# Inverses on distinct values by small DRAM transfers, two additions by accumulating transfers, output weights in one load

## Chip, cores and metric

One NeuronCore of a Trainium2 chip runs the whole kernel. The metric is the device time of one launch in microseconds, as the median over runs. Everything is computed in float32 (apart from a few bfloat16 helpers that carry a shift exactly).

## What is computed

One transformer block with conditioned RMS norms, and its input added once more at the end. x is 4 x 1024 x 512 (4 batches, 4096 tokens), cond is 4 x 128; 16 heads of 32.

```python
def norm(x, t, gw, gb, bw, bb):          # g and b come from the condition
    g = (t @ gw.T + gb)[:, None, :]
    b = (t @ bw.T + bb)[:, None, :]
    return g * x * rsqrt(mean(x * x, -1) + 1e-6) + b

a = norm(x, cond, g1w, g1b, b1w, b1b)
q, k, v = a @ Wq.T, a @ Wk.T, a @ Wv.T   # 16 heads of 32
p = softmax(q @ k.T / sqrt(32))
x2 = x + (p @ v) @ Wo.T
f = norm(x2, cond, g2w, g2b, b2w, b2b)
h = x2 + (silu(f @ gate_w.T) * (f @ hid_w.T)) @ out_w.T
out = x + h
```

## The kernel before, in words

**Layout.** Features lie on the 128 partitions (C = 4 chunks of 128), tokens along the free axis. The 4096 tokens are 8 blocks of 512; a batch is two blocks. A group hg of four heads fills 128 partitions.

**Rounds and units.** The main loop (`while g < NR + 10 ...`) runs rounds g. 256 of them begin a piece of attention: a *unit* j is 256 queries of one head group, and takes UN = 4 rounds, in each of which the scores of 256 keys are made. A block has 8 units, so 32 rounds. `kind` is g % 4. The pieces of one unit follow each other through later rounds: in round r `scores` writes PSUM (one buffer of four banks) and `keep` copies it to SBUF on ACT (tile raw, 9 buffers); `running_max` on DVE; after the fourth, `max_T` (PE, same PSUM buffer as scores), `parts`, `parts_T`, the copy mT on ACT and `spread` turn the maximum over keys into a tile `shift`. Five rounds after r, `shifted` (DVE) and `exponential` (ACT) make the weights; six rounds after, `weighted` multiplies them with v on PE into one PSUM tile av, and `accumulate` adds raw to the unit's first raw by a DMA issued on POOL (three per unit, 1 MB each). So for the last piece of a unit exponential is in kind 0 and accumulate in kind 1. `take_av` copies av to SBUF on ACT in kind 1; the next unit's `weighted` in kind 2 needs that PSUM tile again. In kind 3 `fold_sum` (DVE, L326) adds the two halves of the accumulated tile and `sums` adds over partitions on PE with a matrix of ones, which leaves each of the four heads' sums repeated on 32 partitions. One round later, in kind 0, `inverse` (DVE reciprocal, L341, 128x256) and `normalize` (L351) make oT.

**Chains.** All projections are cut into *chains*: four chunks accumulated in one PSUM tile of a pool of three, followed by an evict on ACT or DVE. There are 512: keys, queries and values of the next batches, the output projection (`project_out`), and per block 32 hidden chains and 16 contract chains of the feed-forward part. `first` holds the output projections with the round in which they are due, `queue` all others with the earliest round. A credit grows each round by 2.0 up to round BS + 16 and by PACE = 1.6 afterwards; a round takes a chain after `accumulate` and a second one (evicted in the next round) near its end, each where the credit is at least 1, something is due, or kind is 0. So a round has none, one or two chains; what is left when the rounds are over runs at the end without attention beside it.

**Order.** The program order of PE, DVE, ACT and POOL is the order of the calls in the loop. In a round it is: scores, the moved additions, the evict left from the round before, what is pinned to the round, spread, keep, exponential, weighted, accumulate, take_av, first chain, sums, running_max, evict, what is set `between`, max_T and parts in kind 0, second chain, parts_T, what is set `after`. All DMAs but the accumulates are issued on SP.

**Norms.** For a block of activations four squares (ACT), three additions (DVE), a matmul with ones/512 that leaves the mean square repeated on all 128 partitions, a square root (ACT, L124), a reciprocal of 128x512 on DVE (`norm_inverse`, L128), a multiplication per chunk (`norm_scale`, DVE) and the modulation (`norm_mod`, ACT). For batches after the first these are set a few rounds ahead of the round s in which the block's chains begin; for the feed-forward part at g0 + 9 to g0 + 16, where g0 is the first round after the block.

**Output projection.** `project_out` (L357) loads the output weights for two chunks at a time (twice per block, in the tag fw that the feed-forward weights use). Its evict adds the residual (L369, x2) and adds x2 to res (L370), into which the contract chains then add.

Of the kernel before, what the change touches and what calls it, by code (L numbers as in the profile page):

```python
# [10 lines left out]
F32 = mybir.dt.float32  # L11
BF16 = mybir.dt.bfloat16
AF = mybir.ActivationFunctionType
ALU = mybir.AluOpType
# [3 lines left out]
P = 128  # L18
NB = 512
# [5 lines left out]
def tile_cond_transformer_block(  # L25
# [12 lines left out]
    nc = tc.nc  # L38
    NBLK, _, C, _ = x.shape
    B = cond_t.shape[1]  # L40
    D = C * P
# [9 lines left out]
    UN = KT // 2  # L51
    RAW = 9
    PACE = 1.6
    SCALE = 1.0 / math.sqrt(DH)

    const = ctx.enter_context(tc.tile_pool(name="const", bufs=1))
# [34 lines left out]

    kq_s = {(b, hg): tc.dram_tile([P, 2, L], F32, name=f"kqs{b}_{hg}") for b in range(B) for hg in range(C)}
    v_s = [tc.dram_tile([P, C, KT, P], F32, name=f"vs{b}") for b in range(B)]


    columns = [P]

    def mm(dst, w, moving, start: bool, stop: bool):
        n = columns[0]
        for k in range(0, P, n):  # L100
            nc.tensor.matmul(dst[k : k + n, :], w[:, k : k + n], moving, start=start, stop=stop)  # L101
# [6 lines left out]
    def norm_squares(dst, tag: str, k: int):  # L108

        sq = [sb.tile([P, NB], F32, tag="t", name=f"sq{tag}_{2 * k + i}", bufs=3) for i in range(2)]  # L110
        for i in range(2):
            nc.scalar.activation(sq[i], dst[:, 2 * k + i, :], AF.Square)
        if k == 0:
            state[tag] = sb.tile([P, NB], F32, tag="tot", name=f"tot{tag}", bufs=1)
            nc.vector.tensor_tensor(state[tag], sq[0], sq[1], ALU.add)
        else:
            for t in sq:
                nc.vector.tensor_tensor(state[tag], state[tag], t, ALU.add)
# [5 lines left out]
        nc.scalar.activation(inv, pm, AF.Sqrt, bias=eps)  # L124
        state[tag] = inv

    def norm_inverse(tag: str):
        nc.vector.reciprocal(state[tag], state[tag])  # L128

    def norm_scale(dst, tag: str, c: int):  # L130
        nc.vector.tensor_tensor(dst[:, c, :], dst[:, c, :], state[tag], ALU.mult)
# [191 lines left out]

    def fold_sum(j: int):
        t = acc[j]
        nc.vector.tensor_tensor(t[:, :, 0, :], t[:, :, 0, :], t[:, :, 1, :], ALU.add)  # L326

    def take_av(j: int):
        avs[j] = sb.tile([P, HQ], F32, tag="avs", name=f"avs{j}", bufs=2)
# [2 lines left out]
    def sums(j: int):  # L332
        total = ps.tile([P, HQ], F32, tag="w", name=f"sum{j}")
        a = acc.pop(j)
        for i in range(HG):
            nc.tensor.matmul(total[i * DH : (i + 1) * DH, :], ones_sum, a[:, i, 0, :], start=True, stop=True)  # L336
        state["sum", j] = total

    def inverse(j: int):
        rec = sb.tile([P, HQ], F32, tag="rec", name=f"rec{j}", bufs=2)  # L340
# [12 lines left out]
    def load_res(n: int):  # L353
        res[n] = sb.tile([P, C, NB], F32, tag="b", name=f"res{n}", bufs=2)
        nc.sync.dma_start(out=res[n], in_=x[n])

    def project_out(n: int, d: int):  # L357

        if d == 0:
            x2[n] = sb.tile([P, C, NB], F32, tag="a", name=f"x2_{n}", bufs=3)  # L360
        if d % 2 == 0:
            wo[0] = sb.tile([P, C, 2 * P], F32, tag="fw", name=f"wo{n}_{d}", bufs=3)
            nc.sync.dma_start(out=wo[0], in_=vo_w[1][:, :, d * P : (d + 2) * P])
        pp = ps.tile([P, NB], F32, tag="w", name=f"po{n}_{d}")
        for c in range(C):
            mm(pp, wo[0][:, c, d % 2 * P : (d % 2 + 1) * P], oT[n, c], c == 0, c == C - 1)

        def evict():
            nc.vector.tensor_tensor(x2[n][:, d, :], pp, res[n][:, d, :], ALU.add)  # L369
            nc.vector.tensor_tensor(res[n][:, d, :], res[n][:, d, :], x2[n][:, d, :], ALU.add)  # L370

        return evict

    def load_f(n: int, f: int):
        t = sb.tile([P, 2, C, P], F32, tag="fw", name=f"fw{n}_{f}", bufs=3)
# [48 lines left out]
    def pin(g, fn, *a):  # L424
        pinned.setdefault(g, []).append((fn, a))

    def between(g, fn, *a):
        halfway.setdefault(g, []).append((fn, a))

    def after(g, fn, *a):  # L430
        ended.setdefault(g, []).append((fn, a))
# [20 lines left out]
        enqueue(0, (load_wkq, (hg,)), project_kq, (0, hg, 1, 1))  # L452
    for b in range(1, B):
        for half in range(QB):
            s = (len(queue) + 1) // 2
            if s > BS + 8:
                s += 2
            tag = f"a{b}_{half}"
            pin(max(s - 10, 0), load_y, b, half)
            for k in range(2):  # L460
                after(s - 8 + k, lambda b=b, half=half, tag=tag, k=k: norm_squares(y[b, half], tag, k))
            between(s - 6, norm_root, tag)
            after(s - 5, norm_inverse, tag)
            for c in range(C):
                between(s - 4, lambda b=b, half=half, tag=tag, c=c: norm_scale(y[b, half], tag, c))
                after(s - 4 + c // 2, lambda b=b, half=half, c=c: norm_mod(0, b, y[b, half], c))
            for load, fn, a in chains_of(b, half):
                enqueue(s, load, fn, a)
    for n in range(NBLK):
        g0 = (n + 1) * BS  # L470
        pin(g0 - 2, load_res, n)
        for d in range(C):
            first.append((g0 + 8, None, project_out, (n, d)))
        if n < NBLK - 1:
            tag = f"f{n}"
            for k in range(2):
                after(g0 + 9 + k, lambda n=n, tag=tag, k=k: norm_squares(x2[n], tag, k))
            between(g0 + 11, norm_root, tag)
            after(g0 + 13, norm_inverse, tag)
            for c in range(C):  # L480
                after(g0 + 14 + c // 2, lambda n=n, tag=tag, c=c: norm_scale(x2[n], tag, c))
            for c in range(C):
                after(g0 + 15 + c // 2, lambda n=n, c=c: norm_mod(1, n // QB, x2[n], c))
            g1 = g0 + 17
        else:
            g1 = 1 << 20
        for g in range(NF // FG):
            for k in range(FG):
                for a in range(2):
                    load = None if a else (load_f, (n, g * FG + k))  # L490
                    enqueue(g1, load, hidden, (n, g * FG + k, a))
            for d in range(C):
                enqueue(g1, None, contract, (n, g, d))
# [23 lines left out]
    with tc.manual_schedule(  # L517
# [32 lines left out]
                modulation(1)  # L550
        project_kq(0, 0, 0, 1)()

        late = None
        credit = 0.0
        g = 0
        while g < NR + 10 or pinned or ended:
            kind = g % UN
            r_x, r_v = g - UN - 1, g - UN - 2
            x_on, v_on = 0 <= r_x < NR, 0 <= r_v < NR
            j_m = g // UN - 1  # L560
            m_on = 0 <= j_m < NR // UN
            j_s = g // UN - 2
            s_on = 0 <= j_s < NR // UN
            j_n = g // UN - 3
            n_on = 0 <= j_n < NR // UN
            columns[0] = DH

            if g < NR:
                scores(g)
            if kind == 3 and s_on:  # L570
                fold_sum(j_s)
            if x_on and kind in (2, 3):
                shifted(r_x)
            if late is not None:
                late()
                late = None
            if kind == 0:
                if n_on:
                    inverse(j_n)
                if x_on:  # L580
                    shifted(r_x)
                if n_on:
                    normalize(j_n)
            for fn, a in pinned.pop(g, []):
                fn(*a)
            if kind == 1 and m_on:
                spread(j_m)
            if g < NR:
                keep(g)
            if kind == 1 and x_on:  # L590
                shifted(r_x)
            if x_on:
                exponential(r_x)
            if v_on:
                weighted(r_v)
                accumulate(r_v)
            if kind == 1 and s_on:
                take_av(j_s)
            credit = min(credit + (2.0 if g < BS + 17 else PACE), 2.9)
            due = bool(first) and first[0][0] <= g  # L600
            evict = None
            if credit >= 1 or due or kind == 0:
                evict = chain(g)
                credit -= evict is not None
            if kind == 3 and s_on:
                sums(j_s)
            if g < NR:
                running_max(g)
            if evict is not None:
                evict()  # L610
            if kind == 3 and g < NR:
                fold_max(g // UN)
            for fn, a in halfway.pop(g, []):
                fn(*a)
            if kind == 0 and m_on:
                columns[0] = P
                max_T(j_m)
                parts(j_m)
            if credit >= 1 or due or kind == 0:
                late = chain(g)  # L620
                credit -= late is not None
            if kind == 0 and m_on:
                parts_T(j_m)
            columns[0] = DH
            for fn, a in ended.pop(g, []):
                fn(*a)
            g += 1
# [63 lines left out]
```

## Time and profile before

| | us |
|---|---|
| median of 3 runs | 2547.93 (2547.44 to 2548.41) |
| the profiled execution: its own time | 2551.1 |
| its span, first to last instruction | 2549.3 |
| rounds begin, about | 48 |
| last scores begin | 2244 |

| groups on DVE that the change touches | count | mean ns |
|---|---|---|
| L341 reciprocal 128x256 | 64 | 1749 |
| L128 reciprocal 128x512 | 7 + 6 | 3345 |
| L326 fold of sums | 64 | 1214 |
| L370 res + x2 | 32 | 692 |

| transfers | count | KB | us from issue to landing, median |
|---|---|---|---|
| accumulate, issued on POOL | 192 | 1024 | 8.4 |
| fw, on SP | 128 | 512 | 4.2 |
| wo, on SP | 16 | 512 | 5.2 |
| out, on SP | 32 | 256 | 3.3 |
| condT, on ACT, at the start | 1 | 2 | 3.8 |

PE works in every slice of the span; the other engines' busy times are shares beside it. Shares are averages over a start (about 50 us), a stage in which the projections of later batches fill the rounds (to round 46), the blocks after it, and an end of about 240 us with the chains that are left. PE's gaps (the time between the end of all its matmuls so far and the next) and the stretches of half clock are read from single records; the waits say what ended them.

### The profile page before, as it was taken

The page shows a single profiled execution, that of the slowest core. Times are in us where ns is not written, and L with a number is a line of the kernel's source. Part 1 is how long each engine was busy: PE and PEld are TensorE (multiplying, and loading weights), DVE is VectorE, ACT ScalarE, POOL GpSimd, SP SyncE. Part 2 cuts the span into 40 slices and gives each one's busy share as a digit, 9 for nine tenths or more (in the row PEclk, how much of TensorE's full clock was granted, in tenths as well). Part 3 has the DMA queues.
Part 4 walks back from the last instruction along what each step waited for, and adds up shares of the span by engine and source line. Part 5 has one row for each costly group of instructions (what it writes and reads, how often), then busy time and mean ns, then how long its engine had stood idle before and what let it go on. Part 6 is the DMA issues. An engine that isn't in the chain of part 4 may idle for free. (4 is left out here: it accounts for less than half of the span.)

```text
span 2549.3 us, 51152 instructions
## 1 busy us (share of the span) xinstructions
PE 2473.6 (97%) x22976; PEld 1003.2 (39%) x22976; DVE 1803.1 (71%) x1600; ACT 1311.6 (51%) x1165; POOL 166.4 (7%) x200
## 2 busy tenths in 40 slices
PE   8999999999999998999999999999999999999999
PEld 3334344334433443344434433344334433433444
DVE  2566766777878787888887888788887878763211
ACT  3566775655555554655565555555555555541000
POOL 0000000000000000000000000000000000000000
PEclk9999999999999999999999999999999999999999
DMA  5678778767767775877677766877677766772221
GB/s 193 181 195 218 211 194 207 182 143 165 174 163 203 164 168 137 203 174 175 164 176 186 177 155 168 197 170 166 152 197 167 174 160 171 165 164 78 90 80 49
DMA packets 125931, 424.08 MB, mean 166 GB/s; under 512 B 12176, under 2 KB 36752, under 8 KB 99216
## 3 DMA queue, kind: packets, MB, share of 16 engines
q0 software_dynamic: 27648, 201.34, 41.0%
q1 hardware_dynamic: 97776, 219.45, 25.7%
q8 instruction: 181, 2.97, 0.5%
q14 instruction: 38, 0.31, 0.0%
q10 hardware_dynamic: 288, 0.01, 0.0%
HBM read 185.87 MB, written 33.55 MB: 86 GB/s over the span
## 5 line engine op out<-in xcount | busy, mean ns | idle before, releaser
L101 PE MATMUL ph<-x,fw 128*32 128x512 f32 (+1 forms) x6488 | 918.5, 595 | 6.7 <-DVE h L393 2.9
L289 DVE TENSOR_TENSOR raw<-raw,shift 128x2048 f32<-128x2048 f32 x256 | 581.3, 2271 | 108.8 <-ACT shift L285 108.8
L237 ACT COPY raw<-sc 128x2048 f32<-128x2048 f32 x256 | 479.4, 1873 | 320.8 <-PE sc L230 184.1
L294 ACT ACTIVATE raw<-raw 128x2048 f32<-128x2048 f32 x256 | 490.0, 1914 | 259.5 <-DVE raw L289 259.3
L101 PEld LDWEIGHTS ph<-x,fw 128*32 128x32 f32 (+1 forms) x6488 | 298.4, 118 | 511.6 <-issue 474.6
L101 PE MATMUL pc<-h,ow 128*32 128x512 f32 (+1 forms) x3184 | 460.6, 595 | 7.8 <-DVE h L395 5.4
L247 DVE TENSOR_TENSOR rmax<-rmax,raw 128x2048 f32<-128x2048 f32 x128 | 292.9, 2288 | 89.7 <-ACT raw L237 88.8
L318 POOL DMA_DIRECT2D raw<-raw x192 | 165.3, 861 | 2124.6 <-ACT raw L294 1303.3
L230 PE MATMUL sc<-kq 32*128 32x256 f32 x4096 | 295.3, 402 | 2.6 <-ACT raw L237 2.6
L304 PE MATMUL av<-raw,v 128*32 128x256 f32 x4096 | 277.8, 389 | 9.3 <-ACT raw L294 6.9
L101 PEld LDWEIGHTS pc<-h,ow 128*32 128x32 f32 (+1 forms) x3184 | 149.9, 118 | 259.8 <-issue 231.9
L230 PEld LDWEIGHTS sc<-kq 32*128 32x128 f32 x4096 | 185.9, 185 | 168.1 <-issue 132.7
L101 PE MATMUL pkq<-y,wkq 128*32 128x512 f32 (+1 forms) x1808 | 233.6, 600 | 9.6 <-DMA wkq<-in_kq_w 5.5
L393 DVE SCALAR_TENSOR_TENSOR h<-t,ph 128x512 f32<-128x512 f32 x128 | 88.0, 687 | 190.6 <-ACT t L391 190.6
L391 ACT ACTIVATE t<-ph 128x512 f32<-128x512 f32 x128 | 75.4, 589 | 219.9 <-PE ph L101 219.9
L407 DVE SCALAR_TENSOR_TENSOR res<-pc,res 128x512 f32<-128x512 f32 x128 | 88.0, 688 | 107.0 <-PE pc L101 106.9
L245 DVE TENSOR_TENSOR rmax<-raw,raw 128x2048 f32<-128x2048 f32 x64 | 146.2, 2285 | 24.4 <-ACT raw L237 24.4
L304 PEld LDWEIGHTS av<-raw,v 128*32 128x32 f32 x4096 | 108.2, 110 | 135.3 <-issue 48.7
L395 DVE TENSOR_TENSOR h<-ph,h 128x512 f32<-128x512 f32 x128 | 88.0, 688 | 68.8 <-PE ph L101 68.5
L101 PEld LDWEIGHTS pkq<-y,wkq 128*32 128x32 f32 (+1 forms) x1808 | 71.5, 115 | 143.2 <-issue 123.9
L101 PE MATMUL po<-oT,wo 128*32 128x512 f32 (+1 forms) x856 | 117.5, 605 | 10.2 <-DMA wo<-in_vo_w 6.0
L275 ACT COPY mT<-pt 12x256 bf16<-12x256 bf16 x64 | 23.1, 361 | 196.7 <-PE pt L273 196.7
(78 smaller groups left out, 1369.1 us busy)
## 6 DMA issues: line engine op xcount, KB each, us to landing
raw<-raw POOLq DMA_DIRECT2D x192, 1024.0 KB, 8.4
fw<-in_gh_w SPq DMA_DIRECT2D x128, 512.0 KB, 4.2
ow<-in_out_w SPq DMA_DIRECT2D x128, 256.0 KB, 4.8
wkq<-in_kq_w SPq DMA_DIRECT2D x32, 512.0 KB, 7.0
v<-vs SPq DMA_DIRECT2D x32, 512.0 KB, 5.8
kq<-kqs SPq DMA_DIRECT2D x31, 512.0 KB, 7.8
kqs<-st SPq DMA_DIRECT2D x61, 256.0 KB, 6.1
res<-in_x SPq DMA_DIRECT2D x8, 1024.0 KB, 6.5
```

Of the source, the lines that this page charges most:

```text
L101: nc.tensor.matmul(dst[k : k + n, :], w[:, k : k + n], moving, start=start, stop=stop)
L230: nc.tensor.matmul(sc[:, i, k, :], t[rows, kt * P : (kt + 1) * P], t[rows, q0 : q0 + HQ], start=True, stop=True)
L237: nc.scalar.copy(raw[r], state.pop(("sc", r)))
L245: nc.vector.tensor_tensor(rmax[j], raw[r - 1], raw[r], ALU.max)
L247: nc.vector.tensor_tensor(rmax[j], rmax[j], raw[r], ALU.max)
L289: nc.vector.tensor_tensor(t, t, shift[r // UN].unsqueeze(2).to_broadcast([P, HG, 2, HQ]), ALU.add)
L294: nc.scalar.activation(raw[r], raw[r], AF.Exp)
L304: nc.tensor.matmul(av[j][i * DH : (i + 1) * DH, :], v[m][:, kt, i * DH : (i + 1) * DH], raw[r][:, i, k, :], start=(kt == 0), stop=(kt == K ...
L318: nc.gpsimd.dma_start(out=acc[j].rearrange("p h k q -> p (h k q)"), in_=raw[r].rearrange("p h k q -> p (h k q)"), accum_op=ALU.add,)
L393: nc.vector.scalar_tensor_tensor(h[n, f], t, 1.0, pp, ALU.add, ALU.mult)
L395: nc.vector.tensor_tensor(h[n, f], pp, h[n, f], ALU.mult)
L407: nc.vector.scalar_tensor_tensor(r, pp, 0.5, r, ALU.mult, ALU.add)
```

## The change

The reciprocals are no longer taken on tiles in which each value is repeated on 32 or 128 partitions. Instead `compact` writes one row per head (or one row in all) to DRAM, `take` reads these values back spread over 128 partitions (8 or 4 per partition), `invert` takes their reciprocal on DVE, `put` writes them to DRAM, and `spread_inverse` reads them back repeated (four transfers for a unit, one for a norm). All of these are issued on ACT. For a unit, the sums are first copied from PSUM by ACT (kind 3), taken in kind 0 before keep, inverted and put at the end of kind 0, spread in kind 1 ahead of take_av, and `normalize` moves from kind 0 to kind 2. The last unit keeps the direct reciprocal, as do the first two norms and the last one.

`fold_sum` becomes an accumulating transfer on POOL in kind 2, behind `accumulate`. The addition of x2 to res becomes one accumulating transfer per block on POOL (`add_res`), but for the last block. The output weights of blocks 1 to 7 are loaded whole, seven rounds ahead, into tag a (three buffers, shared with y and x2). The credit grows by FIRST = 1.75 instead of 2.0, up to three rounds longer; output projections are due two rounds later, norms begin earlier ahead of s or later after g0, and feed-forward chains are let in at g0 + 20 instead of g0 + 17.

```diff
...
     PACE = 1.6
+    FIRST = 1.75
     SCALE = 1.0 / math.sqrt(DH)
...
     v_s = [tc.dram_tile([P, C, KT, P], F32, name=f"vs{b}") for b in range(B)]
+    inv_s = {}
...
-    def norm_inverse(tag: str):
-        nc.vector.reciprocal(state[tag], state[tag])
+    def compact(tag: str, t, rows: int, n: int):
+        inv_s[tag] = tc.dram_tile([P // rows, n], F32, name=f"sums{tag}")
+        nc.scalar.dma_start(out=inv_s[tag], in_=t[0:P:rows, :])
+    def take(tag: str):
+        src = inv_s.pop(tag)
+        few = sb.tile([P, src.shape[0] * src.shape[1] // P], F32, tag="few", name=f"few{tag}", bufs=2)
+        nc.scalar.dma_start(out=few, in_=src.rearrange("h (p c) -> (h p) c", c=few.shape[1]))
+        state["few", tag] = few
+    def invert(tag: str):
+        few = state["few", tag]
+        nc.vector.reciprocal(few, few)
+    def put(tag: str):
+        few = state.pop(("few", tag))
+        inv_s[tag] = tc.dram_tile(list(few.shape), F32, name=f"invs{tag}")
+        nc.scalar.dma_start(out=inv_s[tag], in_=few)
+    def spread_inverse(tag: str, t, rows: int, n: int):
+        src = inv_s.pop(tag).rearrange("(h p) c -> h (p c)", p=rows)
+        for h in range(P // rows):
+            nc.scalar.dma_start(
+                out=t[h * rows : (h + 1) * rows, :], in_=src[h : h + 1, :].to_broadcast([rows, n])
+            )
+    def norm_compact(tag: str):
+        compact(tag, state[tag], P, NB)
+    def norm_spread(tag: str):
+        spread_inverse(tag, state[tag], P, NB)
...
         t = acc[j]
-        nc.vector.tensor_tensor(t[:, :, 0, :], t[:, :, 0, :], t[:, :, 1, :], ALU.add)
+        nc.gpsimd.dma_start(out=t[:, :, 0, :], in_=t[:, :, 1, :], accum_op=ALU.add)
...
+    def sums_out(j: int):
+        t = sb.tile([P, HQ], F32, tag="rec", name=f"total{j}", bufs=2)
+        nc.scalar.copy(t, state.pop(("sum", j)))
+        compact(f"s{j}", t, DH, HQ)
+    def sums_in(j: int):
+        t = sb.tile([P, HQ], F32, tag="rec", name=f"rec{j}", bufs=2)
+        spread_inverse(f"s{j}", t, DH, HQ)
+        state["rec", j] = t
     def inverse(j: int):
...
+    def load_wo(n: int):
+        t = sb.tile([P, C, D], F32, tag="a", name=f"wo{n}", bufs=3)
+        nc.sync.dma_start(out=t, in_=vo_w[1])
+        for d in range(C):
+            wo[d] = t[:, :, d * P : (d + 1) * P]
     def project_out(n: int, d: int):
...
             x2[n] = sb.tile([P, C, NB], F32, tag="a", name=f"x2_{n}", bufs=3)
-        if d % 2 == 0:
-            wo[0] = sb.tile([P, C, 2 * P], F32, tag="fw", name=f"wo{n}_{d}", bufs=3)
-            nc.sync.dma_start(out=wo[0], in_=vo_w[1][:, :, d * P : (d + 2) * P])
+        if n == 0 and d % 2 == 0:
+            t = sb.tile([P, C, 2 * P], F32, tag="fw", name=f"wo{n}_{d}", bufs=3)
+            nc.sync.dma_start(out=t, in_=vo_w[1][:, :, d * P : (d + 2) * P])
+            for i in range(2):
+                wo[d + i] = t[:, :, i * P : (i + 1) * P]
         pp = ps.tile([P, NB], F32, tag="w", name=f"po{n}_{d}")
         for c in range(C):
-            mm(pp, wo[0][:, c, d % 2 * P : (d % 2 + 1) * P], oT[n, c], c == 0, c == C - 1)
+            mm(pp, wo[d][:, c, :], oT[n, c], c == 0, c == C - 1)
...
             nc.vector.tensor_tensor(x2[n][:, d, :], pp, res[n][:, d, :], ALU.add)
-            nc.vector.tensor_tensor(res[n][:, d, :], res[n][:, d, :], x2[n][:, d, :], ALU.add)
+            if n == NBLK - 1:
+                nc.vector.tensor_tensor(res[n][:, d, :], res[n][:, d, :], x2[n][:, d, :], ALU.add)
         return evict
+    def add_res(n: int):
+        nc.gpsimd.dma_start(
+            out=res[n].rearrange("p c q -> p (c q)"),
+            in_=x2[n].rearrange("p c q -> p (c q)"),
+            accum_op=ALU.add,
+        )
...
         for half in range(QB):
-            s = (len(queue) + 1) // 2
-            if s > BS + 8:
+            s = math.ceil((len(queue) + 1) / FIRST)
+            if s > BS + 11:
                 s += 2
             tag = f"a{b}_{half}"
-            pin(max(s - 10, 0), load_y, b, half)
+            pin(max(s - 11, 0), load_y, b, half)
             for k in range(2):
-                after(s - 8 + k, lambda b=b, half=half, tag=tag, k=k: norm_squares(y[b, half], tag, k))
-            between(s - 6, norm_root, tag)
-            after(s - 5, norm_inverse, tag)
+                after(s - 9 + k, lambda b=b, half=half, tag=tag, k=k: norm_squares(y[b, half], tag, k))
+            between(s - 7, norm_root, tag)
+            between(s - 7, norm_compact, tag)
+            after(s - 7, take, tag)
+            between(s - 6, invert, tag)
+            after(s - 6, put, tag)
+            between(s - 5, norm_spread, tag)
             for c in range(C):
...
         pin(g0 - 2, load_res, n)
+        if n:
+            pin(g0 + 3, load_wo, n)
         for d in range(C):
-            first.append((g0 + 8, None, project_out, (n, d)))
+            first.append((g0 + (10 if n < NBLK - 1 else 8), None, project_out, (n, d)))
         if n < NBLK - 1:
             tag = f"f{n}"
+            after(g0 + 12, add_res, n)
             for k in range(2):
-                after(g0 + 9 + k, lambda n=n, tag=tag, k=k: norm_squares(x2[n], tag, k))
-            between(g0 + 11, norm_root, tag)
-            after(g0 + 13, norm_inverse, tag)
+                after(g0 + 12 + k, lambda n=n, tag=tag, k=k: norm_squares(x2[n], tag, k))
+            between(g0 + 14, norm_root, tag)
+            between(g0 + 14, norm_compact, tag)
+            after(g0 + 14, take, tag)
+            between(g0 + 15, invert, tag)
+            after(g0 + 15, put, tag)
+            between(g0 + 16, norm_spread, tag)
             for c in range(C):
-                after(g0 + 14 + c // 2, lambda n=n, tag=tag, c=c: norm_scale(x2[n], tag, c))
+                after(g0 + 17 + c // 2, lambda n=n, tag=tag, c=c: norm_scale(x2[n], tag, c))
             for c in range(C):
-                after(g0 + 15 + c // 2, lambda n=n, c=c: norm_mod(1, n // QB, x2[n], c))
-            g1 = g0 + 17
+                after(g0 + 18 + c // 2, lambda n=n, c=c: norm_mod(1, n // QB, x2[n], c))
+            g1 = g0 + 20
         else:
...
+        direct = NR // UN - 1
         late = None
...
                 scores(g)
-            if kind == 3 and s_on:
-                fold_sum(j_s)
             if x_on and kind in (2, 3):
...
             if kind == 0:
-                if n_on:
+                if n_on and j_n >= direct:
                     inverse(j_n)
...
                 if n_on:
-                    normalize(j_n)
+                    if j_n >= direct:
+                        normalize(j_n)
+            if kind == 2 and n_on and j_n < direct:
+                normalize(j_n)
+            if kind == 0 and n_on and j_n < direct:
+                take(f"s{j_n}")
             for fn, a in pinned.pop(g, []):
...
                 accumulate(r_v)
+            if kind == 2 and s_on:
+                fold_sum(j_s)
+            if kind == 1 and n_on and j_n < direct:
+                sums_in(j_n)
             if kind == 1 and s_on:
                 take_av(j_s)
-            credit = min(credit + (2.0 if g < BS + 17 else PACE), 2.9)
+            credit = min(credit + (FIRST if g < BS + 20 else PACE), 2.9)
             due = bool(first) and first[0][0] <= g
...
                 sums(j_s)
+                if j_s < direct:
+                    sums_out(j_s)
             if g < NR:
...
                 parts_T(j_m)
+            if kind == 0 and n_on and j_n < direct:
+                invert(f"s{j_n}")
+                put(f"s{j_n}")
             columns[0] = DH
```

## Prediction

> **What bounds the kernel now.** I read the page first: which engine is full, and when.
>
> ```profile
> PE 2473.6 (97%) x22976; PEld 1003.2 (39%) x22976; DVE 1803.1 (71%) x1600; ACT 1311.6 (51%) x1165; POOL 166.4 (7%) x200
> ...
> PE   8999999999999998999999999999999999999999
> ...
> PEclk9999999999999999999999999999999999999999
> DMA  5678778767767775877677766877677766772221
> ```
>
> PE is busy 97% of the span of 2549.3 us and the change takes no matmul away, so only PE's empty time (71 us, its gaps added up) and clock lost after gaps (27 us, from the granted clock) can be won: 98 us. Next the windows, to see where these lie.
>
> ```profile
> 448.00:512.00 64.00, 58.58 (x610) 23.57 (x598) 49.64 (x39) 40.42 (x39) 4.30 (x5) 0.96 0.73 184
> ...
> 960.00:1024.00 64.00, 57.06 (x570) 22.72 (x567) 47.07 (x44) 33.53 (x27) 4.31 (x5) 0.95 0.58 130
> 1088.00:1152.00 64.00, 64.00 (x660) 26.33 (x656) 50.06 (x46) 35.80 (x29) 5.16 (x6) 1.00 0.76 176
> ```
>
> Columns: window, length, busy PE, PEld, DVE, ACT, POOL, clock, DMA share, GB/s. An ordinary stretch (the third) has no PE gap at all, though DVE is at 78%: there a faster DVE wins nothing. Gaps sit in the first 140 us, around round 48 (first line) and at block starts. The waits of PE and PEld name what ends them:
>
> ```profile
> PE pt L273 <- DVE split L268: 13.7, 9, 4.0
> PE po L101 <- DMA wo<-in_vo_w: 6.0, 1, 6.0
> ...
> PEld av L304 <- ACT avs L330: 16.7, 37, 2.0
> ```
>
> The last one is short each time but comes in 37 of 64 units: ACT's copy of avs is already just in time. The timelines of ACT, PE and POOL around one such round (kind 1, one chain) show it:
>
> ```profile
> 1194.63 1.92 ACT L294 ACTIVATE raw<-raw 128x2048 f32<-128x2048 f32 x1 [0.58 <-DVE raw L289]
> 1196.45 0.35 ACT L330 COPY avs<-av 128x256 f32<-128x256 f32 x1
> ...
> 1196.85 1.07 PE L304 MATMUL av<-raw,v 128*32 128x256 f32 x16
> ...
> 1170.91 0.86 POOL L318 DMA_DIRECT2D raw<-raw  x1 [13.74 <-ACT raw L294]
> 1179.23 0.86 POOL L318 DMA_DIRECT2D raw<-raw  x1 [7.46 <-ACT raw L294]
> 1188.46 0.86 POOL L318 DMA_DIRECT2D raw<-raw  x1 [8.37 <-DMA raw<-raw]
> ```
>
> The av starts 0.05 us after the copy ends, and POOL issues three accumulates per unit, each 8.4 us to landing. Last the packets: an accumulate's first packet runs 1.43 us after issue and its packets fill the engines 5.2 us when alone, 6.2 in the median. Of 199 SP transfers with nothing of SP's in front of them, 89 would have begun inside such a run; every one landed after the run's end. The other 110 took 3.5 us in the median, the smallest stores 2.3 (0.82 to the first packet, 0.66 after the last). **An accumulate shuts other transfers out**, and three fill some 60% of a unit.
>
> **The change, part by part** (us of PE time; gains negative).
>
> *Reciprocals, fold, residual off DVE.* 63 x 1.749 + 13 x 3.345 + 64 x 1.214 + 28 x 0.692 = 251 us, less 76 tiny reciprocals at 0.17 (the 128x8 rows): 238 of 1803. It counts where PE's gaps end on DVE: outside the items below, 20 us of gaps at block starts name DVE (split, h, res) and two dips in the clock (3.4 us at half) add 3.4: **-23**. Bounds 0 and -35 (all gaps there).
>
> *FIRST and the later due rounds.* Counting the credit rule through: before, rounds 47 and 48 find the queue empty (7.3 us of gaps and 13.65 us at half clock, 6.8): **-14**, bounds 0 and -14. Rounds without a chain are 74 and 234 before (kind 2, 3.4 each: 1.03 + 0.66 + half of 3.4); after, they are 10 (kind 2) and 109, 141, 173, which are kind 1, where avs has no slack: a missing chain of 3.6 uncovers some 3.3 and a dip adds 1.7. 3.4 + 3 x 5 - 6.8 = **+12**, bounds 5 and 25. 73 chains instead of 63 are left for the end, where one takes 3.43 instead of 3.62: **-2**.
>
> *Output weights whole*, seven rounds ahead: the one wait of 6.0 and its dip of 3.4 go, **-9** (bounds 0, -9).
>
> *take at kind 0.* ACT waits for compact's landing; behind it stand keep, exp and later mT. From the end of sums: copy and handover 0.6, first packet 0.82, landing 0.95, take's issue 0.5 (ACT's two transfers at the start held it 0.41 and 0.47): keep can start at 2.9, or 1.5 after the end of an accumulate that is running. Now it starts 1.2 after sums when kind 3 has one chain, 4.6 when it has two, and max_T comes 2.4 after keep's end; so 3.6 or 7.0 is free. Laid on the recorded accumulates, 16 of 61 units overrun, the longest by 5.5, together **+35**. Bounds 0 (accumulates do not block ACT's row) and 70 (take's read blocked as well).
>
> *put and four spread transfers before avs.* put goes out behind mT, usually into the third accumulate, and lands up to 4 us after kind 1's exp has begun. Four issues of 0.4 then stand in front of take_av; exp hides 1.8 of them. 36 of 62 units have no slack. Laid on the records: 26 units, together **+35**; bounds 0 and 70. At SP's shortest issue, 0.33, it is 6 less.
>
> *Dips.* Of these 42 waits 12 are over 2.2 us, and in the trace most gaps from 2.2 us on are followed by 3.4 us or more at half clock: **+20**, bounds 0 and 40.
>
> *fold_sum and add_res on POOL.* The third accumulate lands 4.3 to 22.4 us ahead of sums, 12 in the median. fold needs 1.43 to its first packet, half the bytes of an accumulate in pieces of 1 KB, some 3, and 0.7: 5.5 to 7.5, which overruns 2 or 3 units by 1.4 to 5.5 in all; if issuing grows fourfold with its 512 pieces, 10 us and some 20. The next accumulate stands behind it on POOL, with 14 us between them. add_res goes ahead of a third accumulate seven times (5.2 us, still inside 12). **+8**, bounds 1 and 30.
>
> *Norms' small transfers*: keep is held up to 6 us after the square root, but the next scores leave it 5.0 to 7.0. **0**; with that cover gone, 13 x 3. The copy out of sums holds the evict behind it on ACT by some 0.6 us and frees a PSUM buffer a round sooner: 0, covered by the three buffers. normalize waits on DVE for the spreads until about 10 us after kind 1 begins, where DVE comes to it anyway (shifted of kind 2 ends about there): 0. load_wo adds no transfer to SP's queue, it merges two: 0.
>
> Sum: -23 - 14 + 12 - 2 - 9 + 35 + 35 + 20 + 8 = **+62**. The profiled execution would have a span of 2611; the runs' median (2547.9) is 1.4 under the span before, so **2610**.
>
> A rule against my step: the Trainium skill, "DMA: Bandwidth & Descriptors", section "Queues, rings and completion order", has each engine go round-robin between queue rows packet by packet. Read with one 8 KB piece as a packet, a small transfer would wait one piece and my +90 would be near nothing, the sum near 2520. The 89 waits above say that a whole accumulate acts as one; the page allows up to 64 descriptors in a packet, which fits.
>
> **Rivals.**
>
> *The chain of small transfers stays hidden*, and the kernel is faster. For it: ACT is idle half the time, and in two-chain rounds keep has 7.0 us. Against: the 89 waits. Without the 90 us the sum is -23 - 14 + 12 - 2 - 9 + 8 = -28: **2520**. It decides at compact's landing: under 3.1 us after sums in one-chain rounds this case holds, beyond it the first.
>
> *POOL and the transfers become the bound*, slower still. Per unit three accumulates of 8.4 and a fold issued in 3.4 make 28.7 of the 31 to 40 that a unit lasts, and the DMA share in the first 450 us is already up to 0.87 with folds adding 0.08. fold's +20 in place of 8, and 3 us in each of 13 units of the first stage: 2610 + 12 + 39 = **2661**. Against: the DMA share in the middle is 0.74.
>
> *Nothing measurable*: some 45% of the waits I laid out come true and cancel the gains: **2548**.
>
> **How the numbers follow.** First case 0.55, hidden 0.25, POOL bound 0.15, nothing 0.05. A measurement here tells 0.2% (5 us) from no change. Faster 0.25, same 0.05, slower 0.70. The first case's own range is 2565 to 2655; the whole, reaching to the hidden case and the upper bounds of the waits, 2515 to 2690.
>
> **What would show it.** Right: PEld av <- ACT avs grows from 16.7 us to over 50, PE mt <- ACT raw L237 from 5.1 to over 20, ACT's raw L237 is ended by the sums transfer, more dips in the clock, no gap near round 48, DVE near 1570 busy. Wrong: take's wait under 3 us in most units, or PE's gaps under 70 us in all; or sums waiting for the fold in most units, which is the POOL case.

## The result, and the profile after

The changed kernel takes **2803.0 us** in the median of four runs (2796.39 to 2826.37) against 2547.68 (2544.99 to 2548.41) for the kernel before in the same session: a ratio of 1.1015 with a 95% interval of 1.0958 to 1.1071. The sign is that of the forecast; the size is not: 2610 was named, and the upper end of the range, 2690, lies 113 us below the time. The profiled execution is the longest of the four (2826.4, span 2823.5); its numbers are compared with the span of before, 2549.3.

The page first, the rows that answer to those of before:

```profile
PE 2553.7 (90%) x22688; PEld 1035.9 (37%) x22688; DVE 1586.2 (56%) x1508; ACT 1334.2 (47%) x1228; POOL 256.3 (9%) x271
...
PEclk9999999999999998999999999999898999999999
DMA  5789997987778777777778877877777767782221
```

DVE is relieved as forecast: 1586, where 1570 was named. But PE, which set the time, has fallen from 97% to 90% of a longer span, and its own busy time has grown by 80 us though it has 288 fewer matmuls: they ran longer, at a lower clock. The windows say how much lower; columns as before (length, busy PE, PEld, DVE, ACT, POOL, clock, DMA share, GB/s):

```profile
448.00:512.00 64.00, 54.07 (x477) 20.80 (x478) 32.07 (x33) 33.91 (x35) 6.46 (x7) 0.92 0.78 184
...
1151.00:1215.00 64.00, 54.58 (x512) 21.79 (x507) 38.70 (x37) 30.03 (x26) 6.92 (x7) 0.95 0.81 194
```

The second is an ordinary stretch with two chains or one in every round; before, such a one had no gap and a clock of 1.00. Now PE does nothing for 9 of 64 us.

One sum holds for every kernel of this study. Take PE's gaps (all time between the end of its matmuls so far and the next) and half of the half-clock time that lies outside those gaps ("lost clock"); what is left of the span is the same in all of them, 2456 us within 3 (2463 in one), whatever the change did to the other engines:

| kernel | span | gaps | lost clock | rest |
|---|---|---|---|---|
| before | 2549.3 | 71.4 | 22.3 | 2455.6 |
| after | 2823.5 | 265.8 | 101.8 | 2455.9 |

So all of the 274 us between the two profiles is PE's: 194 of waiting, 80 of half clock, in 48 stretches against 10. The waits of PE, PEld and ACT name what was waited for (total, times, longest):

```profile
PE av L338 <- ACT avs L364: 110.5, 45, 6.7
PE mt L291 <- ACT raw L271: 65.7, 22, 4.8
PE sc L264 <- ACT raw L271: 25.0, 7, 7.1
...
ACT raw L271 <- DMA sumss<-total: 184.4, 41, 8.0
...
PEld av L338 <- ACT avs L364: 132.0, 50, 7.1
...
ACT avs L364 <- DMA rec<-invss: 80.8, 29, 5.7
```

Before, these were:

```profile
PE mt L257 <- ACT raw L237: 5.1, 4, 2.1
...
PE sc L230 <- ACT raw L237: 2.6, 3, 1.0
PE av L304 <- ACT avs L330: 2.5, 5, 1.1
```

So the first three alone make 191 of the 194. ACT's rows give the other half of the story: keep (L271) stands behind take, which waits for compact's landing, and avs (L364) stands behind the four spread transfers, which wait for put's.

The timeline of ACT over one unit shows both (start, length; "ACTq" is ACT issuing; in brackets the idle time before and what ended it):

```profile
1181.15 0.50 ACTq L132 DMA_DIRECT2D sumss<-total  x1
1182.92 0.60 ACT L451 ACTIVATE t<-ph 128x512 f32<-128x512 f32 x1 [3.06 <-PE ph L103]
1186.99 0.34 ACTq L138 DMA_DIRECT2D fews<-sumss  x1
1187.43 1.87 ACT L271 COPY raw<-sc 128x2048 f32<-128x2048 f32 x1 [3.91 <-DMA sumss<-total]
...
1194.08 0.34 ACTq L148 DMA_DIRECT2D invss<-fews  x1
...
1198.73 1.91 ACT L328 ACTIVATE raw<-raw 128x2048 f32<-128x2048 f32 x1 [0.58 <-DVE raw L323]
1203.82 1.80 ACTq L154 DMA_DIRECT2D rec<-invss  x4
1205.66 0.37 ACT L364 COPY avs<-av 128x256 f32<-128x256 f32 x1 [5.02 <-DMA rec<-invss]
```

POOL and PE over the same unit:

```profile
1179.48 0.86 POOL L352 DMA_DIRECT2D raw<-raw  x1 [7.50 <-DMA raw<-raw]
1191.40 0.86 POOL L352 DMA_DIRECT2D raw<-raw  x1 [11.06 <-ACT raw L328]
```

```profile
1206.08 1.93 PE L338 MATMUL av<-raw,v 128*32 128x256 f32 x16 [5.09 <-ACT avs L364]
1207.79 6.55 PE L103 MATMUL ph<-x,fw 128*32 128x512 f32 x52
```

compact goes out 1.7 us after an accumulate (L352, 1179.48) and lands some 5 us later; only then take and keep. put goes out 2.7 us after the next accumulate (1191.40), so the first spread transfer is issued at 1203.82, 5.1 us after exp began, and avs is copied 5 us late. PE waits those 5 us, and the av that follows takes 1.93 us instead of 1.07: half clock.

### The profile page after: what moved, and what is told of

The parts are those of the page before. It is cut to its first block, busy times and chain, and to the rows that moved or that the text cites. A ratio compares the mean times of both kernels' runs of the same rounds, so it can differ in the third digit from the quotient of the medians.

```text
span 2823.5 us, 51642 instructions
## 1 busy us (share of the span) xinstructions
PE 2553.7 (90%) x22688; PEld 1035.9 (37%) x22688; DVE 1586.2 (56%) x1508; ACT 1334.2 (47%) x1228; POOL 256.3 (9%) x271
## 4 chain that ended last, share of the span: by engine, by line
PE 62%; DMA 23%; ACT 7%; ACTq 3%; DVE 3%; issue 2%; DVEq 0%; SPq 0%
PE ph L103 24%; PE pc L103 12%; DMA invss<-fews 7%; PE av L338 6%; DMA sumss<-total 6%; PE pkq L103 5%; PE sc L264 5%; PE po L103 3%; DMA fews<-sumss 3%; PE pv L103 3%; ACTq L154 3%; PE mt L291 2%; DMA rec<-invss 2%; DVE raw L323 2%; ACT raw L271 2%
## 5 line engine op out<-in xcount | busy, mean ns | idle before, releaser
L103 PE MATMUL ph<-x,fw 128*32 128x512 f32 (+1 forms) x6200 | 947.6, 610 | 12.9 <-DVE h L453 6.2
L271 ACT COPY raw<-sc 128x2048 f32<-128x2048 f32 x256 | 479.3, 1872 | 403.1 <-DMA sumss<-total 184.4
L103 PEld LDWEIGHTS ph<-x,fw 128*32 128x32 f32 (+1 forms) x6200 | 312.3, 123 | 536.5 <-issue 497.4
L103 PE MATMUL pc<-h,ow 128*32 128x512 f32 (+1 forms) x3112 | 475.8, 612 | 11.7 <-DVE h L455 6.5
L338 PE MATMUL av<-raw,v 128*32 128x256 f32 x4096 | 293.4, 407 | 124.0 <-ACT avs L364 110.5
L352 POOL DMA_DIRECT2D raw<-raw x192 | 166.3, 866 | 1697.4 <-ACT raw L328 1013.6
L338 PEld LDWEIGHTS av<-raw,v 128*32 128x32 f32 x4096 | 111.2, 113 | 258.2 <-ACT avs L364 132.0
L291 PE MATMUL mt<-ident,rmax 128*128 128x128 f32 x512 | 82.2, 312 | 65.7 <-ACT raw L271 65.7
L360 POOL DMA_DIRECT2D raw<-raw x64 | 82.9, 1296 | 552.5 <-DMA raw<-raw 519.8
```

Of the source, the lines that this page charges most:

```text
L271: nc.scalar.copy(raw[r], state.pop(("sc", r)))
L291: nc.tensor.transpose(pt[:, qt, i, :], rmax[j][:, i, 0, qt * P : (qt + 1) * P], ident)
L338: nc.tensor.matmul(av[j][i * DH : (i + 1) * DH, :], v[m][:, kt, i * DH : (i + 1) * DH], raw[r][:, i, k, :], start=(kt == 0), stop=(kt == K ...
L352: nc.gpsimd.dma_start(out=acc[j].rearrange("p h k q -> p (h k q)"), in_=raw[r].rearrange("p h k q -> p (h k q)"), accum_op=ALU.add,)
```

## The experiments

Each is an edit of the changed kernel, but for the last. "Wait" rows are PE's.

**The units' inverse back on DVE**, everything else as changed:

```diff
-        direct = NR // UN - 1
+        direct = 0
```

> The unit sums are inverted by the DVE reciprocal again (sums straight from PSUM, inverse and normalize in kind 0); norms, fold, add_res, output weights and FIRST stay as in the changed kernel. Theory A (ACT waits in order for small transfers that stand behind accumulates, PE waits for ACT and loses clock): the waits av <- avs (110 us) and mt <- keep (66 us) and most of the 104 us of extra half clock go, 2530 to 2580 us; the scores' wait for keep (25 us, norms) stays. Rival B (the added accumulating transfers and DMA load are the cost): stays above 2720. Rival C (the norms' transfers carry most of it): stays above 2700.

2571.4 us, ratio 1.0105 [1.0085, 1.0125]; gaps 78.0, lost clock 30.8. The two big waits are gone:

```profile
PE av L338 <- ACT raw L328: 13.8, 10, 2.1
PE sc L264 <- ACT raw L271: 10.5, 6, 2.2
PE sum L370 <- DMA raw<-raw: 7.0, 5, 3.3
PE av L338 <- ACT avs L364: 6.5, 6, 1.9
PE mt L291 <- ACT raw L271: 6.1, 4, 3.0
```

232 of the 255 us are the units' seven small transfers. POOL has the same folds and accumulates in this kernel, so the case in which POOL becomes the bound is out as the main cause.

**The norms' inverse on DVE too** (`norm_compact` to `norm_spread` leave; `norm_inverse` as before at s - 6 and g0 + 16):

> As the run before, and the norms' inverses by the DVE reciprocal as well: no small transfer is left; fold and residual by accumulating transfers, whole output weights and FIRST remain. Theory A: 2500 to 2530 us, faster than the kernel before, clock loss under 25 us. Rival B: above 2700. If the scores' waits for keep (25 us and their half clock) come from the norms' transfers, this is 30 to 50 us under the run before.

2549.9 us, ratio 1.0007 [0.9993, 1.002]. The norms are worth 21 us (2571.4 to 2549.9), not nothing. What they cost shows in unit_direct in the rounds after compact (offsets are rounds after g0): keep of offset 15 stands behind the norm's take, which waits for compact to land.

```profile
ACT raw L271 <- DMA sumsf<-invf: 41.0, 7, 6.7
```

The scores of offset 16 wait for that keep, and av for the exponential behind it: 10.7 us in rounds 48, 80, 112, 144 and 208. In round 239 DVE's running maximum waits for it too, and pc 5.0 us behind DVE. And the rest, which was to bring some 28, brings nothing: the time lies above the 2500 to 2530 expected. Two runs below take this apart.

**Only the norms' inverse on DVE**, the units' as changed:

> The changed kernel with the norms' inverses by the DVE reciprocal again; the units' small transfers stay. Theory A: the scores' waits for keep of 6 to 7 us at block starts go (25 us) with the half clock after them, 2730 to 2775 us. Rival C (norms carry most): under 2650.

2762.7 us, ratio 1.0841 [1.0822, 1.0861]: 40 us less than the changed kernel, so beside the units' transfers the norms' cost about twice what they cost alone. Av still waits 102.8 us for avs and mt 46.3 for raw.

**The accumulates left out:**

```diff
-        else:
-            nc.gpsimd.dma_start(
-                out=acc[j].rearrange("p h k q -> p (h k q)"),
...
-            )
```

> Leaves out the three accumulating transfers of raw per unit, so the sums hold a quarter of the keys; all else as in the changed kernel. Theory A with accumulates as what delays the small transfers: their last packets come within 2 us of issue in most cases, av <- avs under 25 us, mt <- keep under 15 us, clock loss under 50 us, 2520 to 2600 us. Rival D (the fixed time of four transfers in a row is too long by itself): av <- avs and mt <- keep stay above 100 us together, time above 2700.

2535.7 us, one run; gaps 61.6, lost clock 16.9. All small transfers are issued as before, in the same places, and PE waits little for them:

```profile
PE av L338 <- ACT avs L358: 19.7, 24, 2.2
PE sc L264 <- ACT raw L271: 8.5, 4, 2.4
```

So ACT's issuing and the length of the chain of transfers cost little by themselves (19.7 us of waits for avs, against 2.5 before); what costs is the accumulates beside them. The packets agree: from issue to last packet compact took 4.38 us in the median of the changed kernel and 1.27 here, take 3.52 and 1.26, put 4.89 and 1.04, a spread transfer 3.06 and 1.63. How much a kernel without small transfers would win if the accumulates were left out was not tried.

**The order on ACT:** take behind exp, the spreads behind avs' copy.

```diff
-            if kind == 0 and n_on and j_n < direct:
-                take(f"s{j_n}")
...
                 exponential(r_x)
+            if kind == 0 and n_on and j_n < direct:
+                take(f"s{j_n}")
...
-            if kind == 1 and n_on and j_n < direct:
-                sums_in(j_n)
             if kind == 1 and s_on:
                 take_av(j_s)
+            if kind == 1 and n_on and j_n < direct:
+                sums_in(j_n)
```

> All small transfers stay; on ACT, take is moved behind keep and exponential of kind 0, and the four spread transfers behind take_av of kind 1. Theory A (it is the place in ACT's program order, not the transfers as such): av <- avs falls from 110 us to under 15, mt <- keep from 66 to under 15, 2540 to 2620 us. Rival B (transfers and DMA load as such): above 2700.

2695.7 us, ratio 1.058 [1.0547, 1.0613]. The waits it was to remove are nearly gone, and it recovers 107 us, but far less than the 2540 to 2620 expected; others have come:

```profile
PE av L338 <- ACT raw L328: 32.4, 21, 2.4
PE sc L264 <- ACT raw L271: 29.2, 10, 7.6
PE ph L103 <- DVE h L453: 17.9, 10, 5.5
PE pc L103 <- DVE h L455: 12.9, 4, 5.4
PE po L103 <- DVE oT L395: 12.3, 6, 5.3
PE mt L291 <- ACT raw L271: 10.8, 8, 2.2
PE av L338 <- ACT avs L364: 8.0, 11, 1.2
```

```profile
DVE oT L395 <- DMA rec<-invss: 137.5, 46, 10.3
...
DVE fews L143 <- DMA fews<-sumss: 102.4, 38, 6.5
```

The values now come so late that DVE, in order too, stands at invert and at normalize, and the chains behind them (ph, pc, po) wait for its evicts; before the move these two waits of DVE were 117.9 and 44.0. 19.7 us of sc's wait are the three rounds in which no chain covers it (those behind 109, 141, 173): there ACT stands at put until invert is done, invert stands until take has landed, and keep comes after put in either order.

**All small transfers issued on SP instead of ACT** (`nc.scalar.dma_start` becomes `nc.sync.dma_start` in compact, take, put and spread_inverse):

> The changed kernel with the same small transfers at the same places of the program, issued on SP instead of ACT, so that SP and not ACT stands still until one has landed. Theory A (ACT standing still in order is what PE pays for): av <- avs under 20 us, mt <- keep under 15 us, 2580 to 2700 us; what remains is DVE waiting for values that come late, as in the run with the order changed, and weight loads behind SP's waits. Rival E (that the values come late, whoever waits): time stays above 2750.

2622.6 us, ratio 1.0281 [1.0258, 1.0305]. ACT no longer waits for the small transfers to land, and 180 us return:

```profile
PE ph L103 <- DVE h L455: 18.0, 5, 12.4
PE sc L264 <- ACT raw L271: 14.7, 7, 3.9
PE ph L103 <- DVE h L453: 12.4, 5, 6.5
PE mt L291 <- ACT raw L271: 12.1, 5, 7.5
PE av L338 <- ACT avs L364: 7.0, 6, 1.9
```

Much of what is left is DVE's lateness (ph behind h, 30.4). Take and put are still late, 5.4 and 3.8 us to the last packet in the median: what cost most was that ACT stood behind them.

**The fold back on DVE**, all else as changed:

```diff
-        nc.gpsimd.dma_start(out=t[:, :, 0, :], in_=t[:, :, 1, :], accum_op=ALU.add)
+        nc.vector.tensor_tensor(t[:, :, 0, :], t[:, :, 0, :], t[:, :, 1, :], ALU.add)
```

> The changed kernel with the fold of the two halves back on DVE, in kind 2 where the transfer is issued now. Theory A with the fold as one more accumulate in the way of the spread transfers: av <- avs falls from 110 to 60 to 90 us, 2730 to 2790 us. Rival F (the fold is what holds the spread transfers, not the third accumulate): av <- avs under 40 us, under 2700.

2770.2 us, ratio 1.0866 [1.0845, 1.0888], 33 us less. In the changed kernel the fold runs when the spreads go out: 175 of the 252 spread transfers had packets of an accumulating transfer running between their issue and their own first packet, and one of ACT's four issues then took up to 2.44 us instead of 0.44. Here 42 of 252 have, and av still waits 90.3 us for avs: it is put's late landing, not the spreads' own, that holds most.

**No small transfers, and the fold on DVE** (all_direct with the line above):

> all_direct with the fold of the sums back on DVE (63 folds of 1.2 us). Theory A: the waits of sums for the fold's landing (10.9 us in seven gaps, two of them over 2.2 us and followed by a clock dip, 3.4 us more) are what eats part of DVE's relief; without them the time is 2530 to 2542. Rival B: PE's empty time is set elsewhere and moves when one wait goes; the gap at sums goes to nothing, other gaps (PE pt <- DVE split, DVE h) grow by as much and the time stays within 5 us of all_direct's 2550: 2545 to 2555.

**2531.6 us** (2530.37 to 2537.49), ratio 0.9938 [0.9925, 0.9951]: faster than both kernels. Gaps 56.1, lost clock 16.7; of PE's waits the one for the fold is gone, and none has come for it:

```profile
PE av L341 <- ACT avs L367: 8.0, 6, 1.9
PE sc L267 <- ACT raw L274: 7.8, 4, 2.2
PE pkq L103 <- DMA wkq<-in_kq_w: 5.8, 1, 5.8
PE pt L310 <- DVE split L305: 4.9, 8, 1.5
```

So weights loaded whole, the residual by one transfer and the slower credit together are worth 16 us, and the fold by transfer costs 18 of it back, though it takes 68 us of work off DVE (1783.5 to 1715.5 busy).

**The credit as before** in all_direct (2.0 to round BS + 16):

> all_direct with the credit as before (2.0 to round BS + 16, norms laid by it), the fold on POOL. The slower credit was priced -14 for the empty queue of rounds 47 and 48 and +12 for rounds 109, 141 and 173 without a chain: so within 5 us of all_direct, 2545 to 2555, with the gaps moved: rounds 47 and 48 again 7 us and a dip, rounds 110, 142 and 174 full. Rival: the three rounds of kind 1 or 2 without a chain cost more than the two of the empty queue, and the time falls under 2543; or the other way, over 2557.

2560.8 us, ratio 1.005 [1.0035, 1.0066], over the interval I had given for no effect. Around round 48 it has 8.9 us of gaps and 20.5 us at half clock; and PE waits behind four rounds of kind 1 without a chain (77, 173, 205, 237) as it does behind three in all_direct. Its pt waits 10.6 us for DVE, with DVE at 1714 us. The slower credit is worth 11 us here.

**The useful parts on the kernel before:** weights whole, `add_res` at g0 + 10, FIRST 1.8, PACE 1.65; inverses and fold as before.

> The kernel before with the parts that cost nothing of ACT's order: whole output weights from block 1 on, residual by an accumulating transfer, and the credit set so that by its rule no round of the first 256 is without a chain (FIRST 1.8, PACE 1.65, 59 chains left); inverses and fold stay on DVE. Theory: the gaps of rounds 47, 48, 74 and 234 with their half clock (21 us) and the output weights' wait at block 3 (9 us) go, 2510 to 2530 us. If the gaps only move, 2540 to 2555.

2544.6 us, ratio 0.9984 [0.9974, 0.9994], not the 2510 to 2530 expected. Its gaps, 66.5 us, lie in other rounds than before (31, 41 and 43 are new), and pt waits 11.6 again. The paces and due rounds of the change itself, in direct_fold_dve, are the better ones; which of them makes the difference was not tried.

## Why the prediction was wrong, step by step

**The mechanism was right in the main.** Small transfers are late beside accumulates, ACT waits for them in order, and PE, which has no other work there, waits for ACT. The signs named came but one (rounds 46 and 48 still have 3.2 and 2.4 us of gaps): PEld av <- ACT avs 132.0 us (over 50 was named), PE mt <- ACT raw 65.7 (over 20), ACT's raw ended by the sums' transfer, 38 more dips, DVE at 1586. no_acc shows the accumulates as the cause, sp_issue ACT's waiting as what carried most of it to PE (180 of 255 us).

**The step that failed is "Laid on the records".** I put the new transfers on the accumulates' times of the kernel before, and let one be late where it would begin while an accumulate's packets ran. That gave 35 us in 16 units for take and 35 in 26 for put and spreads. Measured: mt 61 more, and av 108 more in 45 waits.

The pattern came as laid out. In the changed kernel 29 of 63 compacts and 47 of 63 puts would begin (0.82 us after issue) among an accumulating transfer's packets; the layout had 29 of 61 and 46 of 62. But the units of these compacts hold only 27.8 of mt's 65.7 us, and those of these puts 67.5 of av's 110.5. The others are units that this test leaves free. Most of them are compacts and puts (28 and 16) that were due between such a transfer's issue and its first packet, which came up to 5.6 us after issue, not the 1.43 counted on. Of these, 19 and 13 took over 2 us to their last packet. Whether that transfer alone held them is not shown: in no_acc 19 compacts and 29 puts took over 2 us as well. And where put was counted, the price was low: in the 44 waits for avs that can be laid to a unit, the four spread issues took 1.95 us to avs in the median and up to 5.0, where 1.6 was laid down.

Waits that I had left out come on top. That take is late stood in the upper bound alone, and what stands behind it nowhere: DVE waits at invert for take, and ACT at put for invert (the second line is what came next on ACT after six of these puts).

```profile
DVE fews L143 <- DMA fews<-sumss: 44.0, 18, 7.0
...
ACT sqf L114 <- DVE fews L143: 28.0, 6, 5.8
```

In rounds 77, 205 and 237 chains wait for the evicts behind invert, 15.9 us in all, and behind rounds 109, 141 and 173 the scores wait for the keep behind put, 19.3. My upper bounds (70 and 70) came from the same layout, so the range was too narrow with the point.

**Dips: +20, measured +80.** I had 12 waits long enough; 55 gaps are over 2 us (12 before), and there are 48 stretches at half clock for 10. The price of one was right: most last 3.4 or 6.8 us. The number failed with the step above.

**Norms: 0, measured 21 alone and 40 beside the units'.** I had looked at keep alone and found that "the next scores leave it 5.0 to 7.0". That was too much slack: in unit_direct keep stood 5.3 to 6.7 us behind the norm's compact in seven rounds, and PE paid at sc, at av behind the exponential and once at pc, with their dips. Why it costs twice as much beside the units' transfers is open.

**fold_sum and add_res: +8.** The fold alone costs 18: sums waits for its landing in 7 units, 10.9 us in all, where 2 or 3 units were forecast; it lands 6.0 us after issue (5.5 to 7.5 named), and issuing took 1.29 us, not the 3.4 of the bound. The count failed, not the price; the rest of the 18 lies in other gaps and the clock.

**DVE off the path: -23.** Too large. pt's wait for split falls from 13.7 to 3.4 in all_direct, but it is 4.9 in direct_fold_dve, with DVE at 1783, 20 us under before, and 10.6 in direct_credit with DVE at 1714. It follows the pace of the chains, not DVE's total: the gaps that I gave to the reciprocals and the fold were the credit's.

**FIRST and the weights: -4 and -9.** About right together: the parts without fold and inverses come to -16 in the median. The credit is worth more than I gave it, -11 by direct_credit. The rounds without a chain are those counted, 109, 141 and 173; in direct_fold_dve each leaves 3.6 to 3.8 us of gaps and a dip, near the 5 laid down. In the changed kernel sc alone waits 6.6, 5.6 and 7.1 us there, 19.3 of its 25.0, for the keep that is late behind put. The wait for the weights stays at 4.9 us: it is block 0's now, which still loads them in halves.

**The rivals.** "Hidden" (2520) is what no_acc looks like, 2536, when the accumulates are away. "POOL bound" (2661) was the nearer number for the wrong reason: fold_dve takes the fold off POOL and 222 us of the loss stay. The rule that was weighed in the prediction (the Trainium skill, "DMA: Bandwidth & Descriptors", section "Queues, rings and completion order": round-robin between queue rows, packet by packet) would, read as one piece per packet, have left the small transfers nearly free. They were not: the first packet of compact, take and put came 3.9, 2.1 and 3.4 us after issue in the median, 1.2, 1.0 and 0.85 in no_acc. But "a whole accumulate acts as one" does not hold either. In the unit above put's 128 packets came from 1198.74 to 1203.28, among the accumulate's (1196.62 to 1203.26), and compact's began at 1185.66, inside a run from 1182.22 to 1189.20. The packets show that they interleave, not in what turns.

## What to carry to other kernels

Where PE sets the time, count only what PE waits for: 217 us of DVE's work were removed here, and 274 us of waiting and half clock bought with it. A small transfer is cheap alone and costs what it meets: before one is put on an engine that works in order, look up which long transfers share the DMA engines at that moment and what is queued behind the waiting instruction. Do not take a transfer for free because no other's packets would run at its start: one that has been issued and has not begun may count too. Follow a late landing through every engine that waits for it in order, here DVE at invert and ACT at put. Price every such wait at its worst case in every unit as the upper bound, and add the clock behind each.

## What the runs showed of the hardware

**Short gaps cost clock.** Over the twelve profiles, a gap of PE of 0.2 to 1.5 us was followed, within 3.4 us of its end, by a stretch of half clock in 8 of 433 cases, one of 1.5 to 2.0 us in 34 of 102, 2.0 to 2.5 in 54 of 85, 2.5 to 3.5 in 38 of 48, longer ones in 124 of 125. Nearly all stretches last 3.4 us or a multiple of it (3.41, 6.83, 10.24, 13.65), and in each profile all begin on one grid of 3.41 us. Counted by the windows of this grid that ran at full clock, the next window was at half clock after 201 of 204 with 2.0 us or more without a matmul, after 24 of 99 with 1.5 to 2.0, and after 2 of 8478 with less. So it is the idle time in a window that decides, and a gap of 2 to 3 us costs clock or not by where it falls. The Trainium skill, "TensorE: Matmul & The Clock Gate", section "HAM oscillation — how this bites in real kernels", gives the rule as no idle gap over about 3.4 us; the windows of that length agree with these runs, the threshold does not: here it is about 2 us without work in a window.

**An issue can be slow.** ACT's issue of a spread transfer took 0.44 us in the median and up to 2.44 while the fold's accumulate ran. POOL's issue of the fold, with 512 pieces of 1 KB, took 1.29 us against 0.86 for an accumulate with 128 of 8 KB.
